# Keys straight into the split key stack, and the first two query stacks made on chip, in a one-core attention and feed-forward layer

## The chip, the cores and the metric

The kernel runs on one core of a Trainium2 chip. A core has a matrix engine (TensorE, PE in the profile; PEld is its weight load), a vector engine (VectorE, DVE), a scalar engine (ScalarE, ACT), a general engine (GpSimd, POOL) and a queue engine (SyncE, SP) that issues most DMA transfers. Matrix products are written to PSUM, eight banks of 128 partitions by 512 float32 values; everything else on chip lies in SBUF. The metric is the device time of one execution in microseconds (us); lower is better. Several runs of a kernel are told by their median.

## The reference

The input `x` is 4 sequences of 512 tokens with 1024 features. The layer is an attention block and a quantised linear layer, each behind a layer norm and with a residual sum:

```python
q = (ln(x) @ Wq).reshape(b, s, 32, 32)          # 32 heads of 32
k, v = split(ln(x) @ Wkv)                       # one key and one value head for all heads
scores = q @ k.T / sqrt(32) + slope[h] * (pos_k - pos_q)      # causal, -inf above
x = x + softmax(scores) @ v @ Wo
w = (six_bit_codes - zero_point) * scale        # 1024 x 1024
x = x + ln(x) @ w.T + bias
```

## The kernel before, in words

All products take float32 values split in a rounded part and a remainder ("hi" and "lo", type fp32r), so that a product of two values becomes two or three products on PE. ACT makes the rounded part by a copy, DVE the remainder by a subtraction; the helper `split` (L410 to L417) issues both.

A batch is one sequence. For each batch, `layernorm` normalises four token tiles, `chunk` transposes them into eight tiles `xc` of 128 features by 512 tokens and splits these. `keys_values` forms keys and values together: sixteen products into `pkv` (L616), whose partitions 0 to 63 hold the products with the rounded weights and 64 to 127 those with their remainders. It copies them to `y` (L623), transposes `y` back to tokens (L628), adds the two halves (L632, L636), makes three scaled columns of the key part (rounded, rounded, remainder; L643, L650), and transposes those once more (L660) into rows 0 to 95 of the key stack `kst` (L668). The values stay with tokens on partitions, as the right half of `kv`.

The 32 heads go in eight groups of four, one group a step, so 32 steps `i` over four batches. `queries` (L675) makes the 128 query rows of a group from 24 products into `pq` (L682) and splits them into `qh` and `ql`. It stores both to DRAM and loads them back (L420, helper `move`) as a stack `qs`: rows 0 to 31 rounded, 32 to 63 remainder, 64 to 95 rounded, the four heads side by side; rows 96 to 123 are prepared rows of the position bias, loaded from `qr_d`. One product of `qs` and `kst` then gives split scores with bias. `maxima` (L738, L751) forms scores with queries on partitions and takes row maxima on DVE with a custom instruction; sixteen a group. Its result is transposed (L767), split (L773, L778) and put into two more rows of `qs` by DMA. `attention` forms the scores again with keys on partitions (`st`, L819), takes exp on ACT (L829), zeroes the masked triangle on POOL (L838), multiplies with the values (`pav`, L848), sums the exponentials over key tiles on POOL (L860) and over keys on PE (`den`, L877). After all steps, `token_tile` does the output product (`po`, L1047), the second layer norm and the linear layer (`pf`, L1167) for sixteen tiles of 128 tokens.

PSUM's banks are shared out by name: two for `s`, two for `st`, one each for `av`, `den`, `q` and `misc`. `qs` has three buffers, the staging pool `stg` three.

The order of the work is not written out. Each operation is given with a due time (`at`), an estimated cost, and what it reads and writes; `Work.order` runs a list scheduler forward and backward several times over all engines, with a time per DMA and a penalty for shared ports, and the shortest order found is issued. `STEP` is 15.0 us per group in these due times, `T0` 16.0. A changed due time or dependence can therefore move any operation, far from the edit too. Every engine executes its own queue in order, and so does SP.

Of the kernel before, what the change touches and what calls it, by code (L numbers as in the profile page):

```python
# [32 lines left out]
F32 = mybir.dt.float32  # L33
# [5 lines left out]
ALU = mybir.AluOpType  # L39
# [302 lines left out]
def layer_kernel(  # L342
# [55 lines left out]
    def act(at, n, fn, out, ins, sbuf=False):  # L398
        work.op("ACT", at, n / 1.2 + (90.0 if sbuf else 70.0), fn, out, ins)
# [32 lines left out]

    ident = const([P, P], F32, "ident")
    make_identity(nc, ident())
    ident_r = const([P, P], F32R, "ident_r")
    nc.vector.tensor_copy(ident_r(), ident())
    neg_half = const([P, 1], F32, "neg_half")
    nc.gpsimd.memset(neg_half(), -0.5)

# [146 lines left out]
            [xt], [xt, nmr, rstd], sbuf=True,  # L586
        )

    FIRST = ("q", "misc", "s", "s", "st", "st", "av", "den")

    def chunk(at, b, c):

# [18 lines left out]
    def keys_values(at, b):  # L611
        pkv = new("ps_misc", "misc", [P, S], F32, f"pkv_{b}")
        for c in range(KC):
            def two(c=c):
                for s in range(2):
                    nc.tensor.matmul(  # L616
                        pkv(), wkv()[:, c, :], xc[b, c]()[:, s, :],
                        start=(c == 0 and s == 0), stop=(c == KC - 1 and s == 1),
                    )
            pe(at + 0.1 * c, [S, S], two, [pkv], [wkv, xc[b, c]])  # L620
        at += 1.0
        y = new("stg", "stg", [P, S], F32, f"y_{b}")
        act(at, S, lambda: nc.scalar.copy(y(), pkv()), [y], [pkv])  # L623
        tr = new("ps_misc", "misc", [P, NT, P], F32, f"trkv_{b}")
        for t in range(NT):
            pe(
                at + 0.1, [P + 95],
                lambda t=t: nc.tensor.transpose(tr()[:, t, :], y()[:, ts(t, P)], ident()),  # L628
                [(tr, t)], [y],
            )  # L630
        part = new("kv", "part", [P, NT, 2 * HD], F32, f"part_{b}")
        act(at + 0.2, 256, lambda: nc.scalar.copy(part(), tr()[:, :, 2 * HD :]), [part], [tr])  # L632
        t = kv[b] = new("kv", "kv", [P, NT, 2 * HD], F32, f"kv_{b}")
        dve(
            at + 0.3, 256,
            lambda: nc.vector.tensor_tensor(t(), tr()[:, :, 0 : 2 * HD], part(), ALU.add),  # L636
            [t], [tr, part],
        )
        tok = new("kv", "tok", [P, NT, 3 * HD], F32R, f"tok_{b}")
        for i in range(2):  # L640
            act(
                at + 0.4, P,
                lambda i=i: nc.scalar.activation(  # L643
                    tok()[:, :, ts(i, HD)], t()[:, :, 0:HD], AF.Copy, scale=SM_SCALE
                ),
                [(tok, i)], [t], sbuf=True,
            )
        dve(
            at + 0.5, P,
            lambda: nc.vector.scalar_tensor_tensor(  # L650
                tok()[:, :, ts(2, HD)], t()[:, :, 0:HD], SM_SCALE,
                tok()[:, :, 0:HD].bitcast(F32), ALU.mult, ALU.subtract,
            ),
            [(tok, 2)], [t, (tok, 0)], port=True,
        )
        trk = new("ps_misc", "misc", [P, S], F32R, f"trk_{b}")
        for j in range(NT):
            pe(
                at + 0.6, [P],
                lambda j=j: nc.tensor.transpose(  # L660
                    trk()[0 : 3 * HD, ts(j, P)], tok()[:, j, :], ident_r()
                ),
                [(trk, j)], [tok],
            )
        k = kst[b % 2]
        act(
            at + 0.7, S,
            lambda: nc.scalar.copy(k()[0 : 3 * HD, :], trk()[0 : 3 * HD, :].bitcast(F32)),  # L668
            [(k, "k")], [trk],
        )  # L670


    qs = {}

    def queries(at, i):  # L675
        b, g = divmod(i, NG)
        pq = new("ps_q", "q", [P, S], F32, f"pq_{i}")
        hi, lo = wq[g]
        for c in range(KC):
            def three(c=c):  # L680
                for n, (w, s) in enumerate(((hi, 0), (lo, 0), (hi, 1))):
                    nc.tensor.matmul(  # L682
                        pq(), w()[:, c, :], xc[b, c]()[:, s, :],
                        start=(c == 0 and n == 0), stop=(c == KC - 1 and n == 2),
                    )
            h = c // (KC // 2)
            pe(at + 1.3 * c, [S] * 3, three, [pq], [(hi, h), (lo, h), xc[b, c]], more=12.0)
        at += 10.4
        qh = new("q1", "qh", [P, S], F32R, f"qh_{i}")
        ql = new("q1", "ql", [P, S], F32R, f"ql_{i}")  # L690
        split(at, S, qh, ql, pq, qh, ql, pq)

        qs[i] = [(0, GH, new("qs", "qs", [P, GH, S], F32R, f"qs_{i}"))]
        for s, src in enumerate((qh, ql)):
            dma(
                at + 0.6 + 0.7 * s, 262e3,
                lambda s=s, src=src: move(q_d[i % 4, s], src()), [q_i[i % 4][s]], [src],
            )
# [27 lines left out]
    def maxima(at, i):  # L726
# [3 lines left out]
        for n, bank in enumerate(S_BANKS):  # L730
            ps = new("ps_s", "s", [P, S], F32, f"s_{i}_{n}")
            widths = [(t + 1) * P for t, _ in bank]
            places = [sum(widths[:m]) for m in range(len(bank))]

            def products(ps=ps, bank=bank, widths=widths, places=places):
                for (t, h), W, o in zip(bank, widths, places):
                    q, at = part(i, h)
                    nc.tensor.matmul(  # L738
                        ps()[:, o : o + W], q()[0:R_MAX, at, ts(t, P)], k()[0:R_MAX, :W],
                        start=True, stop=True,  # L740
                    )
            pe(
                at + 1.2 * n, widths, products, [ps],
                [(q, r) for q in {part(i, h)[0] for _, h in bank} for r in ROWS] + [k],
                more=5.0,
            )
            for (t, h), W, o in zip(bank, widths, places):
                junk = new("q1", "junk", [P, S], F32, f"junk_{i}_{t}_{h}")
                dve(
                    at + 1.2 * n + 0.3, W,  # L750
                    lambda ps=ps, junk=junk, t=t, h=h, W=W, o=o: nc.vector.tensor_tensor_reduce(  # L751
                        out=junk()[:, :W],
                        in0=ps()[:, o : o + W],
                        in1=mask()[:, S - W :],
                        scale=1.0,
                        scalar=-3e38,
                        op0=ALU.add,
                        op1=ALU.max,
                        accum_out=mx()[:, h * NT + t : h * NT + t + 1],
                    ),  # L760
                    [(mx, (t, h))], [ps], more=125.0,
                )
# [34 lines left out]
    def attention(at, i):  # L797
# [47 lines left out]
        def products(js):  # L845
            for j in js:
                for h in range(GH):
                    nc.tensor.matmul(  # L848
                        pav()[ts(h, HD), j * P :], kv[b]()[:, j, HD:], pr[j]()[:, h, :],
                        start=(j == 0), stop=(j == NT - 1), tile_position=(0, h * HD),  # L850
                    )
        for js, when in (((0, 1), 10.4), ((2, 3), 14.4)):
# [376 lines left out]
    for b in range(B):  # L1229
# [6 lines left out]
        for c in range(KC):  # L1236
            chunk(
                T - 4.0 + 0.5 * c if b == 0 else T - 0.9 * STEP + 1.3 * c - 2.6, b, c
            )
        keys_values(T + 6.0 if b == 0 else T - 1.0, b)  # L1240
        for g in range(NG):
            i = b * NG + g
            at = T0 + i * STEP
            queries(at, i)
            maxima(at + 17.0, i)
            attention(at + 34.0, i)
        invert(T + NG * STEP + 48.0, b)
    E = T0 + STEPS * STEP
    for c in range(KC):
        prep_wo(E - (NG - 1.2 - c) * STEP, c)  # L1250
    for kc in range(KC):
        load_codes(E - 2.0 + 0.5 * kc, kc)
    ffn_rows(E + 6.0, E + 46.0)
    for k in range(B * NT):
        token_tile(E + (-1.0, 11.0, 37.0)[min(k, 2)] + TILE * max(k - 2, 0), k, E + 25.0)

# [43 lines left out]
```

## Time and profile before

| | before |
|---|---|
| median of 3 runs | 827.22 us (826.88 to 828.23) |
| the profiled execution | 825.42 us |
| its span, first to last instruction | 823.5 us |
| PE busy | 795.9 us (97%) |
| DVE busy | 565.5 us (69%) |
| POOL busy | 514.1 us (62%) |
| ACT busy | 372.3 us (45%) |
| PE's share of the chain of waits | 89% |
| DMA queue of SP, share of 16 engines | 57.0% |

The profile is one execution recorded by the hardware. Busy times count instructions of an engine; matmuls are pipelined and their ends are modelled. In the slices the span is cut into 40 equal parts with a digit for the busy share in tenths. The view by stretches gives the same for chosen intervals. The timeline lists instructions by start; in square brackets stand the engine's idle time before an instruction and what ended it. The chain of waits goes back from the last instruction, at each step to what released it.

### The profile page before, as it was taken

What the parts mean: (1) busy time and instruction counts of PE and PEld (TensorE: products, weight loads), DVE (VectorE), ACT (ScalarE), POOL (GpSimd) and SP (SyncE); (2) the same over time, 40 slices, a digit from 0 to 9 for tenths busy, and PEclk for the clock granted to TensorE, in tenths of its full rate; (3) what the DMA queues carried; (4) which work ended last, traced back from release to release, by engine and by line L of the source; (5) the groups of instructions that cost most, each with busy time, mean ns of one, the idle gap of its engine ahead of it and who ended that gap; (6) DMA issues with size and microseconds to landing.
All of it is one profiled execution on the core that took longest, in us unless ns stands there. A gap on an engine that the chain in (4) does not pass through costs nothing.

```text
span 823.5 us, 13425 instructions
## 1 busy us (share of the span) xinstructions
PE 795.9 (97%) x4480; PEld 594.7 (72%) x4480; DVE 565.5 (69%) x1491; ACT 372.3 (45%) x659; POOL 514.1 (62%) x442
## 2 busy tenths in 40 slices
PE   5979999999999999999999999999999999999997
PEld 4756676777676767676775767667888888888885
DVE  7476777388786388777367675644998666666865
ACT  4336575464775445675556564330233323332320
POOL 4337977276787375877489896879465445554333
PEclk9989999999999999999999999999999999999999
DMA  7885853395553387543567966526875755665321
GB/s 223 245 252 154 232 164 91 111 266 188 155 145 100 106 262 211 148 120 111 174 174 194 235 189 208 170 58 171 214 178 158 173 131 129 152 151 137 97 52 51
DMA packets 131796, 133.39 MB, mean 162 GB/s; under 512 B 42964, under 2 KB 93140, under 8 KB 130704
## 3 DMA queue, kind: packets, MB, share of 16 engines
q1 hardware_dynamic: 130912, 129.01, 57.0%
q0 software_dynamic: 816, 3.53, 1.7%
q8 instruction: 35, 0.57, 0.3%
q14 instruction: 33, 0.27, 0.1%
HBM read 85.58 MB, written 39.85 MB: 152 GB/s over the span
## 4 chain that ended last, share of the span: by engine, by line
PE 89%; DVE 4%; DMA 2%; ACT 2%; issue 1%; POOL 1%; SPq 1%; DVEq 0%; ACTq 0%; POOLq 0%
PE po L1047 21%; PE pq L682 21%; PE pf L1167 13%; PE st L819 9%; PE s L738 9%; PE pav L848 8%; PE den L877 4%; PE pkv L616 2%; PE tr L598 2%; DVE junk L751 2%; ACT p L829 1%; POOL p L860 1%; DMA wo_st<-in_L_attn_Wo_dram 1%; DMA qs<-mt 1%; SPq L420 1%
## 5 line engine op out<-in xcount | busy, mean ns | idle before, releaser
L751 DVE CUSTOM_DVE_ANT_0 junk<-s,mask 128x384 f32<-128x384 f32 (+3 forms) x512 | 250.6, 490 | 119.6 <-PE s L738 88.8
L860 POOL TENSOR_TENSOR p<-p,p 128x1536 f32<-128x1536 f32 (+2 forms) x96 | 232.4, 2421 | 16.7 <-PE pav L848 15.0
L829 ACT ACTIVATE p<-st 128x512 f32<-128x512 f32 (+1 forms) x352 | 183.9, 559 | 115.8 <-PE st L819 110.7
L682 PE MATMUL pq<-xc,wqh 128*128 128x512 f32 x512 | 198.5, 405 | 2.3 <-DVE ql L415 1.4
L1047 PE MATMUL po<-woh,aT 128*128 128x512 f32 x512 | 164.8, 391 | 0.0
L838 POOL TENSOR_SCALAR_AFFINE_SELECT p<-p 128x512 f32<-128x512 f32 x128 | 82.2, 647 | 105.1 <-ACT p L829 104.3
L738 PE MATMUL s<-kst,qs 124*128 124x384 f32 (+3 forms) x512 | 127.5, 324 | 3.9 <-DVE mx L751 3.6
L819 PE MATMUL st<-qs,kst 126*128 126x512 f32 (+1 forms) x352 | 127.1, 399 | 3.9 <-ACT p L829 2.9
L1167 PE MATMUL pf<-wf,xT 128*128 128x512 f32 x512 | 121.1, 390 | 0.7 <-DVE xT L415 0.7
L738 PEld LDWEIGHTS s<-kst,qs 124*128 124x128 f32 x512 | 91.5, 189 | 34.2 <-DVE mx L751 8.9
L682 PEld LDWEIGHTS pq<-xc,wqh 128*128 128x128 f32 x512 | 97.7, 191 | 23.8 <-issue 2.7
L1047 PEld LDWEIGHTS po<-woh,aT 128*128 128x128 f32 x512 | 96.1, 188 | 21.7 <-DVE mx L751 0.8
L1167 PEld LDWEIGHTS pf<-wf,xT 128*128 128x128 f32 x512 | 95.8, 188 | 20.9 <-DVE xT L415 1.1
L682 PE MATMUL pq<-xc,wql 128*128 128x512 f32 x256 | 101.8, 398 | 0.1
L1047 PE MATMUL po<-wol,aT 128*128 128x512 f32 x256 | 99.7, 389 | 0.0
L819 PEld LDWEIGHTS st<-qs,kst 126*128 126x128 f32 x352 | 63.5, 190 | 25.7 <-ACT p L829 10.8
L848 PE MATMUL pav<-p,kv 128*32 128x512 f32 (+3 forms) x1024 | 79.9, 436 | 0.0
L848 PEld LDWEIGHTS pav<-p,kv 128*32 128x32 f32 x1024 | 29.6, 109 | 48.8 <-issue 37.6
L1187 POOL TENSOR_TENSOR x<-x,y 128x512 f32<-128x512 f32 x30 | 42.7, 1425 | 27.4 <-DVE y L1178 27.4
L1047 PEld LDWEIGHTS po<-wol,aT 128*128 128x128 f32 x256 | 48.1, 188 | 9.6
L538 POOL TENSOR_SCALAR rstd_f<-mv_f 128x1 f32<-128x1 f32 x16 | 3.9, 244 | 81.7 <-DVE mv_f L533 72.7
L682 PEld LDWEIGHTS pq<-xc,wql 128*128 128x128 f32 x256 | 49.2, 192 | 7.2 <-POOL wql L489 0.6
(92 smaller groups left out, 878.6 us busy)
## 6 DMA issues: line engine op xcount, KB each, us to landing
qs<-q_d SPq DMA_DIRECT2D x96, 256.0 KB
x<-_attn_hidden_states_dram SPq DMA_DIRECT2D x31, 512.0 KB
q_d<-qh SPq DMA_DIRECT2D x32, 256.0 KB
q_d<-ql SPq DMA_DIRECT2D x32, 256.0 KB
at_d<-a SPq DMA_DIRECT2D x32, 256.0 KB
raw<-at_d SPq DMA_DIRECT2D x16, 512.0 KB
raw<-rden_d SPq DMA_DIRECT2D x64, 128.0 KB
out_dram<-x SPq DMA_DIRECT2D x32, 256.0 KB
```

Of the source, the lines that this page charges most:

```text
L682: nc.tensor.matmul(pq(), w()[:, c, :], xc[b, c]()[:, s, :], start=(c == 0 and n == 0), stop=(c == KC - 1 and n == 2),)
L738: nc.tensor.matmul(ps()[:, o : o + W], q()[0:R_MAX, at, ts(t, P)], k()[0:R_MAX, :W], start=True, stop=True,)
L751: lambda ps=ps, junk=junk, t=t, h=h, W=W, o=o: nc.vector.tensor_tensor_reduce(out=junk()[:, :W], in0=ps()[:, o : o + W], in1=mask()[:, S - ...
L819: nc.tensor.matmul(ps()[:, place, :], k()[0:R_ALL, ts(j, P)], q()[0:R_ALL, mine, j * P :], start=True, stop=True,)
L829: lambda ps=ps, own=own, j=j: nc.scalar.activation(pr[j]()[:, own, :], ps(), AF.Exp),
L838: nc.gpsimd.affine_select(out=d, in_=d, pattern=[[0, GH], [1, P]], compare_op=ALU.is_ge, fill=0.0, base=0, channel_multiplier=-1,)
L848: nc.tensor.matmul(pav()[ts(h, HD), j * P :], kv[b]()[:, j, HD:], pr[j]()[:, h, :], start=(j == 0), stop=(j == NT - 1), tile_position=(0, ...
L860: nc.gpsimd.tensor_tensor(d, d, pr[j](), ALU.add)
L877: nc.tensor.matmul(d()[ts(h, HD), :], onesel()[:, g, :], pr[0]()[:, h, :], start=(g == 0), stop=(g == NG - 1), tile_position=(0, h * HD),)
L1047: nc.tensor.matmul(po(), aT[s][1]()[:, c, :], w()[:, ts(n, HALF)], start=(c == 0 and m == 0), stop=(c == KC - 1 and m == 2),)
L1167: nc.tensor.matmul(pf(), xT()[:, s, c, :], wf[c]()[:, ts(n, HALF)], start=(c == 0 and s == 0), stop=(c == KC - 1 and s == 1),)
L1187: (nc.vector if last else nc.gpsimd).tensor_tensor(d, d, y(), ALU.add)
```

## The change

Keys: the two halves of `pkv` are added at once (ACT copies the lower half's partner to partitions 0 to 63, DVE adds), with features still on partitions. From that sum ACT writes the two scaled rounded row blocks of `kst` and DVE the remainder block. The transposes now serve the values alone and are due four microseconds later; the second set of transposes and the fp32r identity are gone. Keys of the first batch are due ahead of its first queries (`T - 1.0` in place of `T + 6.0`).

Queries: for steps 0 and 1 (`DIRECT = 2`) `pq` lies in the banks `av` and `den`, and a new function `stack_here` fills `qs` from it: per head two ACT copies of 32 rows by 512 and one DVE subtraction. The two stores and three loads of those steps go away; the bias rows are loaded earlier. Their scores wait by head rather than for the whole stack, and `maxima` and `attention` of these steps get earlier due times. The banks in which the first batch's `chunk` transposes are reordered to fit. The row loads of the linear layer get earlier due times.

```diff
-    ident_r = const([P, P], F32R, "ident_r")
-    nc.vector.tensor_copy(ident_r(), ident())
...
-    FIRST = ("q", "misc", "s", "s", "st", "st", "av", "den")
+    FIRST = ("av", "misc", "s", "s", "st", "st", "q", "den")
...
-        act(at, S, lambda: nc.scalar.copy(y(), pkv()), [y], [pkv])
...
+        act(at, S, lambda: nc.scalar.copy(y()[0 : 2 * HD], pkv()[2 * HD :]), [y], [pkv])
+        dve(
+            at + 0.1, S,
+            lambda: nc.vector.tensor_tensor(
+                y()[0 : 2 * HD], pkv()[0 : 2 * HD], y()[0 : 2 * HD], ALU.add
+            ),
+            [y], [y, pkv],
+        )
+        k = kst[b % 2]
+        for i in range(2):
+            act(
+                at + 0.2 + 0.2 * i, S,
+                lambda i=i: nc.scalar.activation(
+                    k()[ts(i, HD), :], y()[0:HD], AF.Copy, scale=SM_SCALE
+                ),
+                [(k, i)], [y], sbuf=True,
+            )
+        dve(
+            at + 0.3, S,
+            lambda: nc.vector.scalar_tensor_tensor(
+                k()[ts(2, HD), :], y()[0:HD], SM_SCALE, k()[0:HD, :].bitcast(F32),
+                ALU.mult, ALU.subtract,
+            ),
+            [(k, 2)], [y, (k, 0)], port=True,
+        )
+        tr = new("ps_misc", "misc", [P, NT, 2 * HD], F32, f"trkv_{b}")
         for t in range(NT):
             pe(
-                at + 0.1, [P + 95],
-                lambda t=t: nc.tensor.transpose(tr()[:, t, :], y()[:, ts(t, P)], ident()),
+                at + 4.0, [P + 60],
+                lambda t=t: nc.tensor.transpose(
+                    tr()[:, t, :], y()[0 : 2 * HD, ts(t, P)], ident()[0 : 2 * HD, 0 : 2 * HD]
+                ),
                 [(tr, t)], [y],
             )
...
+        v = kv[b] = new("kv", "kv", [P, NT, HD], F32, f"kv_{b}")
+        act(at + 4.5, P, lambda: nc.scalar.copy(v(), tr()[:, :, HD:]), [v], [tr])
...
+    DIRECT = 2
+
+    def stack_here(at, i, pq):
+        g = i % NG
+        q = new("qs", "qs", [P, GH, S], F32R, f"qs_{i}")
+        qs[i] = [(0, GH, q)]
+        dma(
+            at - 8.0, 229e3, lambda: move(q()[R_BIAS:R_MAX, :, :], qr_d[g]), [(q, "b")], [qr_i[g]]
+        )
+        for h in range(GH):
+            src = ts(h, HD)
             act(
+                at + h, S, lambda h=h, src=src: nc.scalar.copy(q()[0:HD, h, :], pq()[src, :]),
+                [(q, (0, h))], [pq],
+            )
+            dve(
+                at + 0.6 + h, S,
+                lambda h=h, src=src: nc.vector.tensor_tensor(
+                    q()[ts(1, HD), h, :], pq()[src, :], q()[0:HD, h, :].bitcast(F32), ALU.subtract
                 ),
+                [(q, (1, h))], [pq, (q, (0, h))],
+            )
+            act(
+                at + 0.5 + h, S,
+                lambda h=h, src=src: nc.scalar.copy(q()[ts(2, HD), h, :], pq()[src, :]),
+                [(q, (2, h))], [pq],
+            )
 
     def queries(at, i):
         b, g = divmod(i, NG)
-        pq = new("ps_q", "q", [P, S], F32, f"pq_{i}")
+        p = ("av", "den")[i] if i < 2 else "q"
+        pq = new("ps_" + p, p, [P, S], F32, f"pq_{i}")
...
+        if i < DIRECT:
+            stack_here(at, i, pq)
+            return
...
-        keys_values(T + 6.0 if b == 0 else T - 1.0, b)
+        keys_values(T - 1.0, b)
...
-            maxima(at + 17.0, i)
-            attention(at + 34.0, i)
+            first = i < DIRECT
+            maxima(at + (8.0 if first else 17.0), i)
+            attention(at + (22.0 if first else 34.0), i)
...
-    ffn_rows(E + 6.0, E + 46.0)
+    ffn_rows(E + 0.0, E + 34.0)
```

More of the change, by code (lines that the diff above doesn't have):

```diff
@@ L622, in keys_values @@
         y = new("stg", "stg", [P, S], F32, f"y_{b}")
-        act(at, S, lambda: nc.scalar.copy(y(), pkv()), [y], [pkv])
-        tr = new("ps_misc", "misc", [P, NT, P], F32, f"trkv_{b}")
+        act(at, S, lambda: nc.scalar.copy(y()[0 : 2 * HD], pkv()[2 * HD :]), [y], [pkv])
[7 more added lines that the diff above has]
+        k = kst[b % 2]
@@ L625, in keys_values @@
+        tr = new("ps_misc", "misc", [P, NT, 2 * HD], F32, f"trkv_{b}")
         for t in range(NT):
             pe(
-                at + 0.1, [P + 95],
-                lambda t=t: nc.tensor.transpose(tr()[:, t, :], y()[:, ts(t, P)], ident()),
+                at + 4.0, [P + 60],
+                lambda t=t: nc.tensor.transpose(
+                    tr()[:, t, :], y()[0 : 2 * HD, ts(t, P)], ident()[0 : 2 * HD, 0 : 2 * HD]
+                ),
                 [(tr, t)], [y],
             )
-        part = new("kv", "part", [P, NT, 2 * HD], F32, f"part_{b}")
@@ L632, in keys_values @@
[L632 to L637, printed above, removed]
-        )
-        tok = new("kv", "tok", [P, NT, 3 * HD], F32R, f"tok_{b}")
-        for i in range(2):
-            act(
-                at + 0.4, P,
-                lambda i=i: nc.scalar.activation(
-                    tok()[:, :, ts(i, HD)], t()[:, :, 0:HD], AF.Copy, scale=SM_SCALE
+        v = kv[b] = new("kv", "kv", [P, NT, HD], F32, f"kv_{b}")
@@ new lines, in keys_values @@
+        act(at + 4.5, P, lambda: nc.scalar.copy(v(), tr()[:, :, HD:]), [v], [tr])
+    qs = {}
+    DIRECT = 2
[5 more added lines that the diff above has]
+            at - 8.0, 229e3, lambda: move(q()[R_BIAS:R_MAX, :, :], qr_d[g]), [(q, "b")], [qr_i[g]]
+        )
+        for h in range(GH):
+            src = ts(h, HD)
+            act(
+                at + h, S, lambda h=h, src=src: nc.scalar.copy(q()[0:HD, h, :], pq()[src, :]),
[5 more added lines that the diff above has]
+                    q()[ts(1, HD), h, :], pq()[src, :], q()[0:HD, h, :].bitcast(F32), ALU.subtract
@@ L645, in keys_values @@
                 ),
-                [(tok, i)], [t], sbuf=True,
+                [(q, (1, h))], [pq, (q, (0, h))],
             )
[L648 to L663, printed above, removed]
-            )
[L665 to L673, printed above, removed]
+            act(
+                at + 0.5 + h, S,
+                lambda h=h, src=src: nc.scalar.copy(q()[ts(2, HD), h, :], pq()[src, :]),
+                [(q, (2, h))], [pq],
+            )
@@ L743, in maxima @@
                 at + 1.2 * n, widths, products, [ps],
-                [(q, r) for q in {part(i, h)[0] for _, h in bank} for r in ROWS] + [k],
+                [
+                    (part(i, h)[0], (r, h) if i < DIRECT and r != "b" else r)
+                    for _, h in bank for r in ROWS
+                ] + [k],
                 more=5.0,
@@ L848, in products @@
                     nc.tensor.matmul(
-                        pav()[ts(h, HD), j * P :], kv[b]()[:, j, HD:], pr[j]()[:, h, :],
+                        pav()[ts(h, HD), j * P :], kv[b]()[:, j, :], pr[j]()[:, h, :],
                         start=(j == 0), stop=(j == NT - 1), tile_position=(0, h * HD),
```

## The prediction

> **What bounds the kernel now.** The first view is the head of the page: busy shares, then the slices.
>
> ```profile
> PE 795.9 (97%) x4480; PEld 594.7 (72%) x4480; DVE 565.5 (69%) x1491; ACT 372.3 (45%) x659; POOL 514.1 (62%) x442
> PE   5979999999999999999999999999999999999997
> PEclk9989999999999999999999999999999999999999
> ```
>
> TensorE (PE) is busy 97% of the span and the chain of waits gives it 89%, so time can only come from PE work that goes away, from PE idling, or from its clock. The slices put all but a little of the last two into the first three. The view by stretches, cut at the events of the head, sizes them (columns: stretch, its length, PE, PEld, DVE, ACT and POOL busy, granted PE clock, DMA share, GB/s).
>
> ```profile
> 0.00:8.04 8.04, 0.00 (x0) 0.00 (x1) 3.97 (x9) 0.70 (x1) 3.22 (x20) 1.00 0.75 260
> 8.04:16.06 8.02, 6.91 (x32) 6.28 (x33) 6.77 (x14) 4.85 (x8) 4.58 (x9) 1.00 0.86 224
> 16.06:30.00 13.94, 13.94 (x66) 11.54 (x67) 8.84 (x13) 7.73 (x16) 4.45 (x4) 1.00 0.60 162
> 30.00:41.65 11.65, 9.86 (x44) 7.32 (x43) 6.14 (x22) 3.96 (x7) 4.32 (x4) 1.00 1.04 313
> 41.65:60.70 19.05, 13.60 (x48) 9.79 (x49) 14.43 (x51) 7.17 (x11) 7.41 (x13) 0.88 0.90 251
> 60.70:75.00 14.30, 14.30 (x83) 10.30 (x82) 7.86 (x29) 9.67 (x18) 8.29 (x8) 0.92 0.51 117
> ...
> 44.20:45.90 1.70, 0.33 (x2) 0.18 (x2) 1.67 (x6) 0.26 (x1) 0.00 (x0) 0.98 1.04 289
> 45.90:47.60 1.70, 1.70 (x4) 1.41 (x5) 1.70 (x5) 0.00 (x0) 0.24 (x2) 0.50 1.09 298
> 47.60:49.30 1.70, 1.70 (x5) 1.34 (x4) 1.56 (x5) 0.86 (x2) 0.98 (x3) 0.51 1.10 372
> 49.30:51.00 1.70, 1.70 (x9) 1.39 (x8) 0.00 (x0) 0.91 (x1) 1.61 (x4) 1.00 0.97 342
> ```
>
> Before 16.06 PE waits for the input and the layer norm, which the change leaves alone. From 16.06 to 60.70 PE idles 1.79 + 5.45 = 7.24 us; from 60.70 to 75 not at all, and from 75 to 545 only 5.2 us in 470. The clock falls to half for 3.4 us twice (from 45.9, and likewise from 59.5), which costs 1.7 each, 3.4 us. So 7.24 + 3.4 = 10.64 us stand in the head.
>
> Why PE idles there is in the timeline (start, length, engine, line, tile).
>
> ```profile
> 21.83 0.59 ACT L412 CAST qh<-pq 128x512 fp32r<-128x512 f32 x1 [1.58 <-PE pq L682]
> 26.63 0.99 SPq L420 DMA_DIRECT2D qs<-q_d  x2
> 29.58 0.58 ACT L668 CAST kst<-trk 96x512 fp32r<-96x512 f32 x1 [0.94 <-PE trk L660]
> 34.62 0.63 PE L738 MATMUL s<-kst,qs 124*128 124x512 f32 x2
> 35.06 0.69 DVE L751 CUSTOM_DVE_ANT_0 junk<-s,mask 128x512 f32<-128x512 f32 x1 [1.98 <-PE s L738]
> 45.23 0.27 PE L767 MATMUL trm<-ident,mx 128*16 128x128 f32 x1 [1.68 <-DVE mx L751]
> 57.93 0.68 PE L819 MATMUL st<-qs,kst 126*128 126x512 f32 x2
> ```
>
> The first queries are done at 21.8, the keys at 30.2, yet the first scores start at 34.62: the query halves travel to DRAM and back (issues at 22.45 to 28.84). Then VectorE (DVE) takes the maxima of a group in 9.3 us (35.06 to 45.00, 0.69 of other work taken off), during which PE has little else. The second groups of exp products (st) can start only at 57.93. This is the filling of a pipeline that PE bounds once it is full.
>
> **Part by part.**
>
> *Keys.* PE loses the four trk transposes of each batch. The chain gives them 0.24 us, times 4 batches 0.96. The four trkv transposes, 0.44 in the chain, shrink to a 64-row input and 64 columns: between no saving and the 0.24 of trk; I take 0.1 a batch, 0.4. Together 1.36 us of PE work, nearly all in the part where PE is never idle. ACT: y 0.59 stays; part 0.37, two tok 0.30 and kst 0.58 (1.55) become two stack copies of 512 columns (0.59 each) and the value copy (at most 0.37): 1.55 again. DVE: kv 0.43 and tok 0.29 become two 512-column steps of 0.69: +0.66 a batch, hidden by PE in batches 1 to 3 (DVE 69% busy). If that cover were gone it would be 2.6. The identity's second copy (0.56 on DVE at 1.40) lies in a wait for the input: nothing.
>
> *Order of the start.* The x splits end on DVE at 20.2. Keys' sums, two products (0.46) per chunk, then end at about 20.7; DVE's 0.60 a chunk is slower than PE's 0.46, so PE loses between 0 (the first queries fill in) and 1.0; I take 0.5. Then 0.59 + 0.69 + 0.59 + 0.69 and hand-offs: keys stand at 23.4, or at 26.8 if the weight unpacking that DVE runs at 20.11 to 23.58 stays ahead of them. Sums and first queries are 3.63 + 5.73 of PE work from 16.06: 25.4 to 25.9. Either date of the keys is covered by that.
>
> *Query stacks.* No row has a 32x512 copy. The nearest are 16x128 (0.25 us) and 96x512 (0.58); the 128x512 one is 0.59. Length, not partitions, moves these, so 0.59 is taken; the ends are 0.25 and 0.62. A group goes from one ACT copy and one DVE subtraction to eight (4.7 us) and four (2.8 us). Added in two groups: ACT 14 x 0.59 = 8.2, DVE 6 x 0.69 = 4.1 us. ACT is busy 3.96 of 11.65 us at 30 to 41.65, so it hides 8.2 over 25 to 40; queued behind are weight casts (L487), whose products start later. Each head needs only its own rows, so the first scores wait for two ACT copies and one subtraction beside the second: 25.9 + 1.4 = 27.3, bounds 26.7 and 28.5, against 34.62. Ten transfers of 256 KB (2.6 MB, 8 us at the 313 GB/s seen here) leave a stretch with a DMA share of 1.04. The bias-row loads stay, moved up; the second waits on SP for a row block that GpSimd issues at 23.23 and that lands 4.8 later (median). Weight loads queue behind it, needed at about 33: nothing, or up to 3 us if they come that late.
>
> The Trainium skill, PSUM — Partial Sum Buffer, section "PSUM bank collisions raise a hardware error", says two engines must not read one bank and quadrant together. The second ACT copy and the subtraction of a head do just that. No row of this kernel does it; if they were kept apart, the first group would be late by up to 2.8 us (estimate, four subtractions of 0.69), and 7.8 below would be about 5.
>
> *DVE after that.* From 27.3 to the end of the second group's maxima: 2 x 9.3, seven stack subtractions 4.8, two query splits 1.4, small maxima 0.5, statistics of batch 1 6.1 (now at 41.5 to 49.2): 31.4, ending at 58.7, or 52.6 if the statistics wait; before 61.99. PE's supply in those 31.4 us: the rest of the second queries 4.1, three more groups of queries 16.5, two groups of scores 4.8, exp products 2.4, value products 2.4, sums 1.0: 31.2. Supply and DVE's pace just balance, so I leave 2.0 us of idling and one half-clock stretch.
>
> The clock row needs a word. The Trainium skill, TensorE: Matmul & The Clock Gate, section "Why this matters for your kernels", has the clock fall after PE-idle gaps of over some 3 us. Here no gap after 16.06 exceeds 1.68 us, and it fell twice, after 3.4 us with PE busy 0.83 (42.5 to 45.9) and about 2.0 (56.1 to 59.5). By the page the 3.4 us would not be there to win, and the gain would be 6.1; the rows decide.
>
> *The rest.* Later batches keep their order but for the keys; value transposes come 4 us later, with nobody waiting until the value products some 14 us on. The longer life of y holds one staging buffer. Row loads for the feed-forward part come 6 and 12 us sooner in plan; waits on them are 1.2 and 0.7 us off PE. Nothing each; a reshuffled order can move the 5.2 us of later idling by some 1.5 either way.
>
> **Sum.** Of 10.64 us, 0.5 + 2.0 + 1.7 = 4.2 stay: 6.4 gained, plus 1.36: 7.8. The profiled execution took 825.42 (span 823.5), so 817.6; the median of the runs is 1.80 above it: 827.22 - 7.8 = 819.4.
>
> **Rivals.** A: DVE bounds the whole filling. Batch 1's statistics and 4.1 us of subtractions sit ahead of the second maxima, PE idles 5.0 us and both half-clock stretches remain: 8.4 stays, 2.2 + 1.36 = 3.6 gained, 823.6. For it: DVE is busy 14.43 of 19.05 from 41.65. Against: it does 6.14 of 11.65 before, and the statistics are not needed for 60 us.
>
> B, slower: PE waits on DVE in crumbs all along the filling, and the clock gate punishes it. With 8.0 us idle and four half-clock stretches of 1.7, 14.8 is lost in place of 10.64; less 1.36 the time rises 2.8 to 830.0. It decides once idling and clock after 16.06 pass 12.0. For it: two stretches follow a half-idle PE already. Against: that needs more idling than now, from an earlier start.
>
> C, no change: the lead is given back later, to 827. Against: PE idles 1% from 75 to 545, so there is no slack to swallow it.
>
> **Numbers.** Forecast 0.66, A 0.17, B 0.12, C 0.05. A measurement of this kernel tells about 0.2%, 1.65 us, from no change. A ends faster but for 0.02, the forecast always: faster 0.81, same 0.07, slower 0.12. Full recovery, 10.64 + 1.36 = 12.0, gives 815.2, the lower end with a little for order: 815.0. The upper end takes in A and late starts: 826.5.
>
> **What would show it.** Right: first scores at about 27, first exp products before 50, one or no half-clock stretch, PE idle after 16.06 near 2.5 us, no trk rows, 32x512 copies of 0.59. Wrong: scores at 27 but maxima still ending near 62 (A), three or more rows at clock 0.5 (B), new PE idling after 75 (C).

## The result, and the profile after

The change made the kernel slower: a median of 832.82 us (832.05 to 833.5, 4 runs) against 827.05 us for the kernel before in the same session, a ratio of 1.0072 with a 95% interval of 1.005 to 1.0093. The profiled execution took 832.68 us with a span of 830.8 us, 7.3 us more than the span of before.

The head of the page, with busy shares and slices, answers to the first view of the prediction.

```profile
PE 802.8 (97%) x4464; PEld 593.2 (71%) x4464; DVE 588.5 (71%) x1496; ACT 377.3 (45%) x669; POOL 524.9 (63%) x442
PE   5988999999999999999999999999999999999997
PEclk9989899999999999999999999999999999999999
```

PE executes 16 instructions fewer and is busy 6.9 us longer. A second slice of low clock has come, the fifth (83 to 104 us), where the kernel before had none. DVE is busy 23 us longer. The view by stretches tells more; the first four lines have the cuts of the prediction.

```profile
16.06:30.00 13.94, 13.23 (x59) 10.10 (x58) 9.16 (x15) 8.55 (x16) 4.59 (x4) 1.00 0.45 118
30.00:41.65 11.65, 11.28 (x52) 8.41 (x50) 9.47 (x35) 6.99 (x13) 3.00 (x3) 1.00 0.37 89
41.65:60.70 19.05, 15.74 (x70) 11.19 (x69) 12.86 (x43) 10.71 (x21) 5.47 (x7) 0.82 0.55 159
60.70:75.00 14.30, 13.65 (x98) 8.63 (x99) 12.46 (x28) 8.54 (x15) 13.29 (x10) 1.00 0.91 248
75.00:100.00 25.00, 22.14 (x90) 13.43 (x88) 16.18 (x57) 15.24 (x25) 19.13 (x26) 0.86 0.79 216
...
465.00:480.00 15.00, 12.96 (x77) 7.76 (x76) 10.24 (x23) 7.31 (x14) 12.10 (x8) 0.89 0.58 167
```

The same view of the kernel before, for the two later stretches:

```profile
75.00:100.00 25.00, 24.50 (x154) 16.70 (x153) 18.88 (x66) 14.15 (x29) 23.32 (x20) 1.00 0.91 261
465.00:480.00 15.00, 15.00 (x93) 11.06 (x92) 9.97 (x37) 10.56 (x23) 13.81 (x10) 1.00 0.75 211
```

Length less PE's busy time is PE's idle time; the clock column shows the half-clock stretches, which begin at 44.4 (6.8 us long), 81.9, 92.1 and 474.4 (3.4 us each). Half of their length is lost.

| us lost to idling + clock | 16 to 75 | 75 to 165 | 165 to 405 | 405 to 560 | after 560 |
|---|---|---|---|---|---|
| before | 7.2 + 3.4 | 0.9 + 0 | 2.8 + 0 | 1.6 + 0 | 0.7 + 0 |
| after | 5.0 + 3.4 | 3.4 + 3.4 | 1.4 + 0 | 3.9 + 1.7 | 0.5 + 0 |

The head gained 2.2 us; 75 to 165 lost 5.9 and 405 to 560 lost 4.0. The timeline shows what became of the first scores (chosen rows: start, length, engine, line, tile; the idle time before in brackets).

```profile
22.96 0.68 DVE L641 SCALAR_TENSOR_TENSOR kst<-y,kst 32x512 fp32r<-32x512 f32 x1 [0.36 <-ACT kst L634]
24.99 1.16 ACT L673 CAST qs<-pq 32x512 fp32r<-32x512 f32 x2 [0.65 <-PE pq L697]
27.51 0.68 DVE L678 TENSOR_TENSOR qs<-pq,qs 32x512 fp32r<-32x512 f32 x1 [0.64 <-ACT qs L685]
27.53 0.50 PE L756 MATMUL s<-kst,qs 124*128 124x512 f32 x1
28.23 0.58 ACT L673 CAST qs<-pq 32x512 fp32r<-32x512 f32 x1 [0.75 <-DVE qs L678]
40.94 1.17 ACT L673 CAST qs<-pq 32x512 fp32r<-32x512 f32 x2
42.15 0.68 DVE L678 TENSOR_TENSOR qs<-pq,qs 32x512 fp32r<-32x512 f32 x1 [0.89 <-ACT qs L673]
42.89 0.50 PE L756 MATMUL s<-kst,qs 124*128 124x512 f32 x1 [1.20 <-DVE qs L678]
44.66 1.41 DVE L678 TENSOR_TENSOR qs<-pq,qs 32x512 fp32r<-32x512 f32 x2
45.50 1.49 PE L756 MATMUL s<-kst,qs 124*128 124x512 f32 x2 [2.11 <-DVE qs L678]
50.54 0.74 PE L840 MATMUL st<-qs,kst 126*128 126x512 f32 x1
```

Scores start at 27.53 in place of 34.62 and exp products at 50.54 in place of 57.93. But ACT's copies and DVE's subtractions of one PSUM tile go in turns: ACT waits 0.75 behind a subtraction at 28.23, and the subtraction at 42.15 waits 0.89 behind two copies. PE then waits 3.3 us for the subtractions of the second stack, and the clock halves at 44.4. Further on, again in chosen rows:

```profile
60.30 3.60 POOL L881 TENSOR_TENSOR p<-p,p 128x1536 f32<-128x1536 f32 x1
60.48 3.69 DVE L940 TENSOR_SCALAR v<-qw 128x256 int32<-128x256 int32 x1
78.50 0.49 PE L756 MATMUL s<-kst,qs 124*128 124x512 f32 x1 [0.33 <-DVE mx L772]
467.38 3.49 POOL L881 TENSOR_TENSOR p<-p,p 128x1536 f32<-128x1536 f32 x1
467.67 4.28 DVE L415 TENSOR_TENSOR aT<-raw,aT 128x1024 fp32r<-128x1024 f32 x1 [0.74 <-ACT aT L412]
472.61 0.50 PE L756 MATMUL s<-kst,qs 124*128 124x512 f32 x1 [2.03 <-DVE mx L772]
```

Twice a DVE instruction that reads SBUF started just behind a POOL sum and lasted until that had ended: 3.69 us in place of 0.40 (the like unpacking at 60.23) and 4.28 in place of 1.22 (below). After the second PE waits 2.03 us for the maxima queued behind it.

### The profile page after: what moved, and what is told of

Same layout as the page of the kernel before. It is cut to its first block, busy times and chain, and to the rows that moved or that the text cites. A ratio compares the mean times of both kernels' runs of the same rounds, so it can differ in the third digit from the quotient of the medians.

```text
span 830.8 us, 13410 instructions
## 1 busy us (share of the span) xinstructions
PE 802.8 (97%) x4464; PEld 593.2 (71%) x4464; DVE 588.5 (71%) x1496; ACT 377.3 (45%) x669; POOL 524.9 (63%) x442
## 4 chain that ended last, share of the span: by engine, by line
PE 78%; DVE 7%; DMA 6%; POOL 3%; ACT 2%; issue 2%; SPq 1%; DVEq 0%; POOLq 0%; ACTq 0%
PE pq L697 18%; PE po L1068 17%; PE pf L1188 12%; PE st L840 9%; PE s L756 8%; PE pav L869 6%; PE den L898 3%; DVE junk L772 2%; DMA raw<-rden_d 2%; PE pkv L614 2%; PE tr L596 2%; DMA qs<-q_d 1%; DMA qs<-mt 1%; DMA q_d<-ql 1%; POOL raw L1045 1%
## 5 line engine op out<-in xcount | busy, mean ns | idle before, releaser
L697 PE MATMUL pq<-xc,wqh 128*128 128x512 f32 x512 | 201.9, 407 | 0.8 <-DVE xc L415 0.6
L756 PE MATMUL s<-kst,qs 124*128 124x384 f32 (+3 forms) x512 | 129.8, 329 | 8.9 <-DVE mx L772 4.0
L1208 POOL TENSOR_TENSOR x<-x,y 128x512 f32<-128x512 f32 x30 | 52.1, 1738 | 38.4 <-DVE y L1199 38.3
L1119 ACT COPY halves<-x 128x1024 uint16<-128x1024 uint16 x24 | 23.9, 1044 | 64.9 <-DVE x L1089 64.9
```

What stands on the lines that cost most here:

```text
L697: nc.tensor.matmul(pq(), w()[:, c, :], xc[b, c]()[:, s, :], start=(c == 0 and n == 0), stop=(c == KC - 1 and n == 2),)
L756: nc.tensor.matmul(ps()[:, o : o + W], q()[0:R_MAX, at, ts(t, P)], k()[0:R_MAX, :W], start=True, stop=True,)
L1208: (nc.vector if last else nc.gpsimd).tensor_tensor(d, d, y(), ALU.add)
```

## The experiments

The theories named in the expectations: **D**, the new stacks overfill DVE, and its other work is pushed into 60 to 95 us. **R**, later **O**: the planner deals every engine a new order for any edit, and that alone is worth several us. **T**: the turns on the PSUM bank. **P**: the port that DVE and POOL share. Ratios are to the kernel before in the same session, where its median was 826.05 (e1 to e4), 827.67 (e5 to e8), 827.14 (e9 to e12), 827.52 (e13 to e16) and 826.48 (e17, e18).

### Parts of the change: e1, e2, e3

e1 keeps the key path and sends all query stacks by DRAM again, with the old bank order and row dates:

```diff
-    DIRECT = 2
+    DIRECT = 0
...
-    ffn_rows(E + 0.0, E + 34.0)
+    ffn_rows(E + 6.0, E + 46.0)
```

> The kernel before with the new key path and the earlier key date alone; query stacks, their dates and the row loads as before. Theory D (the two direct query stacks fill VectorE's queue, so its other work is pushed into 60 to 95 us and costs the time): no loss here, 825 to 828, since 0.9 us of trk transposes go and no stack subtractions come. Theory R (the order is reshuffled as a whole, and where GpSimd's port-holding operations meet VectorE's is chance): 822 to 833, PE idling and half-clock stretches at other places than in either kernel.

831.74 us, 1.0076 (1.0056 to 1.0095). e2 keeps the two stacks and gives the keys their old path, transposes and dates, and the row loads their old dates (the old key code is left out here):

```diff
...
-        keys_values(T - 1.0, b)
+        keys_values(T + 6.0 if b == 0 else T - 1.0, b)
...
-    ffn_rows(E + 0.0, E + 34.0)
+    ffn_rows(E + 6.0, E + 46.0)
```

> The kernel before with the two direct query stacks and their dates alone; keys by two sets of transposes and due at their old time, row loads as before. Theory D: most of the loss is here, 831 to 835, with VectorE over 85% busy somewhere between 60 and 95 us and PE idle there. Theory R: 822 to 833, with no fixed place of the loss.

837.06, 1.0133 (1.0113 to 1.0152). e3 is the change with the old row dates alone:

```diff
-    ffn_rows(E + 0.0, E + 34.0)
+    ffn_rows(E + 6.0, E + 46.0)
```

> The changed kernel with the old due times of the row loads of the linear layer. These belong to the end of attention, so the first 400 us should not care. Theory D: 830 to 834, with the same loss at 60 to 95 us. Theory R: even this edit moves the order from the start on, so that stalls in the first 120 us change by over 2 us.

836.34, 1.0137 (1.0119 to 1.0155). Every part alone is slower than before, e3 by more than the whole. e1 has no stack on chip, and D gave it 825 to 828; it lost as much as the whole, which D does not explain. e3 has the order of the changed kernel on PE up to 413 us, and there it is 3.0 us ahead, with 3.4 us less lost to the clock; in other order at the end of the attention it lost all of that and more. Such parts can't be added up, so what follows keeps orders fixed.

### Turns and order, first try: e4 to e8

e4 makes the second copy of a head from the first one in SBUF, so that ACT reads the bank once a head:

```diff
-                lambda h=h, src=src: nc.scalar.copy(q()[ts(2, HD), h, :], pq()[src, :]),
-                [(q, (2, h))], [pq],
+                lambda h=h: nc.scalar.copy(q()[ts(2, HD), h, :], q()[0:HD, h, :].bitcast(F32)),
+                [(q, (2, h))], [(q, (0, h))], sbuf=True,
```

> The changed kernel, but the second rounded copy of each head is taken from the first one in SBUF and not from the PSUM tile, so that ScalarE and VectorE need not take turns on one PSUM tile. In the changed kernel a stack takes 24.99 to 32.64, 7.6 us, with 0.75 of ScalarE idling at each turn. Expected of a stack here: about 5 us if the turns were the cost, 7 or more if not. Time: theory D gives 829 to 832 (2 us less waiting in the head); theory R anything from 823 to 835.

825.05, 0.9994 (0.9975 to 1.0014): some 6.5 us recovered, but the planner had dealt a new order too. The first stack took 6.2 us (25.15 to 31.38), where 7.6 stood in the change and 5 were expected without turns. e5 and e6 (e6 with e4's copies) hold the planned dates of the kernel before, with new operations at the dates of those that they replace:

```diff
-    def order(self, rounds=4, passes=6):
+    KEPT = (...)   # the dates of before's plan
+    def order(self):
+        ...        # one forward pass on these dates
```

> The changed kernel with one difference: the list scheduler makes a single forward pass, in which every operation that the kernel before has too gets the priority and the buffer order of the plan of the kernel before, and the 44 new operations those of the ones they replace (keys' sums ahead of the first queries). From about 300 us on the order is then nearly that of before. Theory R (the loss is a worse order far from the edit, above all at the end of attention): the late idling goes and the time falls to 822 to 826. Theory D (VectorE's work in the head): PE idling and half-clock stretches at 60 to 95 us stay, 830 to 833.

844.75, 1.0203 (1.0176 to 1.023), the slowest of all and outside the ranges of both theories. The timeline of e5 shows where part of that goes (its lines are numbered otherwise; L1480 is the subtraction L415):

```profile
555.46 2.54 POOL L2273 TENSOR_TENSOR x<-x,y 128x512 f32<-128x512 f32 x2
557.96 2.38 POOL L1946 TENSOR_TENSOR p<-p,p 128x1024 f32<-128x1024 f32 x1
560.31 2.47 POOL L2231 TENSOR_TENSOR x<-x,rows 128x512 f32<-128x512 f32 x2
...
555.88 9.21 DVE L1480 TENSOR_TENSOR aT<-raw,aT 128x1024 fp32r<-128x1024 f32 x1
565.14 1.22 PE L2133 MATMUL po<-woh,aT 128*128 128x512 f32 x2 [4.93 <-DVE aT L1480]
```

A subtraction of 1.2 us lasted 9.21 while POOL ran one sum after another, and PE waited 4.93. Dates that were good for one set of operations were not good for another here.

> As the order-kept kernel, and the second rounded copy of each head taken from the first in SBUF, so that a stack no longer takes turns on PSUM. If the turns cost 2 to 3 us in the head: 2 to 3 us less than the order-kept kernel, 819 to 824. If PE had other work under them: the same time within 1.5.

831.2, 1.0058 (1.0036 to 1.0081), far below e5 but above the 819 to 824 expected, with a wait of 5.8 us at 582 of PE's `pf` on DVE's `xT`. e7 gives the kernel *before* only the row dates of the change, which adds no work:

```diff
-    ffn_rows(E + 6.0, E + 46.0)
+    ffn_rows(E + 0.0, E + 34.0)
```

> The kernel before with the new due times of the row loads and nothing else: no work is added or removed. Theory R: the order of the end of attention is moved, and the time by 2 to 8 us either way, with no difference in the first 300 us. Theory D: within 1.5 us of before.

830.6, 1.0042 (1.0024 to 1.006): a neutral edit costs 3.5 us. e8 tests D: the statistics of batch 1 read 64 columns in place of 512, with every engine's order that of the changed kernel:

```diff
-                lambda i=i: nc.vector.bn_stats(st()[:, i, :], xt()[:, ts(i, HALF)]),
+                lambda i=i: nc.vector.bn_stats(
+                    st()[:, i, :], xt()[:, i * HALF : i * HALF + (64 if name[:2] == "a1" else HALF)]
+                ),
```

> The changed kernel in exactly its order, but the layer norm statistics of the second batch read 64 columns of each half instead of 512 (about 0.5 us less on VectorE for each of eight, 4 us, at 65 to 88 us in the changed kernel). Theory D: PE's idling at 75 to 95 us (2.5 us) and the two half-clock stretches there (3.4 us) shrink, and 3 to 5 us go. Theory R: under 1.5 us go.

833.11, 1.0072 (1.0049 to 1.0095), as the change. PE waits at 77 to 81 as before, so the length of the statistics is not what holds PE there. D falls for the statistics.

### The same orders, written out: e9 to e12

Here `order` returns a fixed list, so each pair differs in one thing alone:

```diff
+    ORDER = (...)
     def order(self):
+        return [self.ops[n] for n in self.ORDER]
```

> Every engine's instructions stand in exactly the order of the changed kernel (the list of operations is written out in place of the planner); the one edit is that the second ScalarE copy of a head in the two new query stacks reads the first copy in SBUF, not the PSUM sums, so ScalarE no longer takes turns with VectorE's subtraction on the bank. Theory T, the turns cost the time: PE's waits at 42.9 to 45.5 us (3.3 us, all on that subtraction) go to about 1, and with them part of the half-clock stretch of 6.8 us at 44.4: 832.8 falls by 2.5 to 5, to 828 to 830. Theory O, the copy version won 7 us because the planner gave it another order all along: here the order is the changed kernel's, so 831 to 833 stays, with the waits at 77 to 81 us and at 472 us as they were.

> The converse: the order of the version with copies from SBUF (825.05 us) written out for all engines, but the second copies read PSUM again, as in the change. Theory T: the turns come back, PE waits on the subtractions of the second stack grow by 2 to 3 us at 40 to 46 us: 827.5 to 830. Theory O: the order decides, 825 to 826.5. The two kernels with copies from PSUM then differ by order alone (against 832.8), and so do the two with copies from SBUF.

| ratio to before | second copy from PSUM | from SBUF |
|---|---|---|
| order of the change | 1.0072 (1.005 to 1.0093) | e9: 1.0052 (1.0033 to 1.0071) |
| order of e4 | e12: 1.0028 (1.0 to 1.0056) | e4: 0.9994 (0.9975 to 1.0014) |

Across, the turns: 0.0020 and 0.0034, or 1.7 and 2.8 us; the intervals of each pair overlap, the sign is the same. Down, the order: 0.0044 and 0.0058, or 3.6 and 4.8 us; the intervals of the second pair lie apart. So O is shown, and it weighs more. T is likely, but these times alone do not show it: e9 won less than the 2.5 us expected, and PE's waits on the subtractions fell from 3.3 only to 2.7 us, not to 1. In e12 the same waits rose from e4's 1.8 to 3.6. e10 exchanges two neighbouring POOL instructions of the changed kernel at 467 us:

```diff
 # POOL's order
-p<-p,p (sum)    wol<-wo_st,woh
+wol<-wo_st,woh  p<-p,p (sum)
```

> The changed kernel with its order written out, and one pair of GpSimd instructions exchanged near 467 us: the sum of products (3.49 us) that started 0.3 us ahead of VectorE's subtraction aT now stands behind the 1.2 us weight subtraction that followed it. Nothing else moves on any engine. Theory P, the shared port costs the time there: VectorE's subtraction falls from 4.28 to 1.2 to 2.5 us, PE's wait of 2.03 us at 472.6 goes, and the half-clock stretch behind it (1.7 us) with it: 829 to 831. Against it: if PE's wait there has another cause or the time is lost again behind it, 832 to 833.

830.51, 1.0027 (1.0013 to 1.0041), 3.7 us less than the change. In its timeline:

```profile
472.15 1.22 DVE L415 TENSOR_TENSOR aT<-raw,aT 128x1024 fp32r<-128x1024 f32 x1 [0.74 <-ACT aT L412]
472.72 1.81 POOL L487 TENSOR_TENSOR wol<-wo_st,woh 128x512 fp32r<-128x512 f32 x1 [0.83 <-ACT woh L485]
474.50 5.99 POOL L881 TENSOR_TENSOR p<-p,p 128x1536 f32<-128x1536 f32 x2
```

The subtraction takes 1.22 us, and PE has no wait on the maxima behind it. PE's instructions have one order in both kernels, so the two profiles can be set side by side: e10's, the slowest of its executions (834.92), stands 4.5 us behind the change's at 459 us and 0.4 behind at 479. P holds there: one exchange is worth more than half of the whole loss. e11 has e9's copies, this exchange and one near 60 us (a DMA issue ahead of the sum at 60.30):

> The order of the changed kernel, with the second copies from SBUF, the exchange near 467 us, and one more exchange on GpSimd near 60 us: a DMA issue goes ahead of the sum of products (3.60 us) that held VectorE's unpacking for 3.69 us. If turns and port each cost what theories T and P say, the gains add: 2.5 to 5 and 2 to 3.7, so 824 to 828, about the time before the change. The exchange near 60 frees VectorE for 3.3 us; if the waits at 77 to 81 us (1.9 us) come from VectorE being late, they go too; a run with shorter statistics did not move them, so I expect them to stay. Theory O: 829 to 833.

829.95, 1.003 (1.0016 to 1.0043). The exchange at 467 is worth less here than in e10 (0.0022 against e9, intervals overlapping). The one at 60 did not free the unpacking: its record now starts at 59.79, 0.36 us ahead of the sum's, and still lasts 4.11 us. PE waits 1.3 us on maxima behind it, up to 100 us, as before. So what the 3.69 us at 60.48 cost stays open.

### Design or deal: e13, e15, e16

e13 and e16 give e4 and the kernel before the same neutral dates:

```diff
-    ffn_rows(E + 0.0, E + 34.0)
+    ffn_rows(E + 3.0, E + 40.0)
```

> The version with copies from SBUF (825.05 us), with one edit that has nothing to do with the change: the planner is told to load the feed-forward rows 3 and 6 us later (E + 3, E + 40), and so deals out another order from somewhere in the first 100 us on. Theory O (which order the planner deals is worth several us, whatever the edit): 828 to 832. If the version is better by design and its order is not special: within 1.7 us of 825.

> The kernel before with the same neutral edit (E + 3, E + 40 in place of E + 6, E + 46): a second deal of its planner. Theory O: slower than before by 2 to 5 us, 829 to 832, as with the first such edit (830.6). Against it: within 1.7 us of 827.

e13 took 837.82, 1.013 (1.0114 to 1.0145), more than O expected; at 75 to 110 PE waits 2.3 us on `wql` and 1.7 on `wqh`, weight halves that were dealt late. e16 took 828.5, 1.0022 (1.0002 to 1.0043), less than its expectation. e15 makes only the first stack on chip:

```diff
-    DIRECT = 2
+    DIRECT = 1
```

> The version with copies from SBUF, but only the first group's stack is made by ScalarE and VectorE; the second goes by DRAM as before the change (7 ScalarE copies and 3 subtractions fewer at 37 to 46 us). If the second stack's work on VectorE is what holds PE at 41 to 46 us, the idling at 16 to 75 falls below the 4.3 us of that version, to about 3, unless the DRAM way delays the second scores beyond 41. The planner deals a new order, so the total has the spread of theory O: 823 to 831; read the head from its own stretch.

833.07, 1.0069 (1.0054 to 1.0085). Its total is spoilt at 560 to 600 us, where one wait on DVE takes 4.2. At 16 to 75 PE idles 4.5 us, not the 3 expected; but from 75 to 100 it does not idle at all, and at 100 and 165 e15 is the furthest ahead, as the next table shows. The table is an estimate from one profile of each kernel: each PE instruction is credited with the mean start-to-start time of its kind over the profiles, and the entry is how far a kernel is ahead of the one before at that time, in us of PE work. With medians in place of means the entries at 75 move by some 3 us, so small differences should not be read.

| lead at | 45 | 75 | 100 | 165 | 460 | 540 | 600 |
|---|---|---|---|---|---|---|---|
| after | 0.5 | 2.2 | -4.9 | -4.2 | -1.3 | -4.7 | -8.5 |
| e3, old row dates | 0.5 | 3.5 | -3.0 | -1.1 | 0.0 | -1.7 | -11.0 |
| e4, copies from SBUF | 1.0 | 2.5 | -3.0 | -2.8 | 1.9 | 0.3 | -1.0 |
| e13, e4 with neutral dates | 0.9 | 2.0 | -6.2 | -6.1 | -4.1 | -5.2 | -13.4 |
| e15, one stack | 0.2 | 1.4 | 2.8 | 3.8 | 1.3 | -0.8 | -9.9 |
| e7, before, neutral dates | 0.0 | 3.3 | 0.3 | -0.7 | 1.6 | -1.7 | -4.6 |
| e16, before, neutral dates | 0.1 | 3.7 | 1.7 | 2.3 | 4.5 | 1.9 | -3.8 |
| e18, moved by hand | 2.1 | 4.0 | -1.8 | -1.2 | 3.5 | 1.0 | 0.7 |

Two things can be read off. First, all four deals of the whole change lose 5.5 to 8.2 us between 75 and 100, the kernel before in other deals 2.0 and 3.0, and the version with one stack nothing; e2, with both stacks but late keys, fell from 1.5 to 0.1. Counted as idling and clock, these four lose 4.3 to 9.1 us there, e1 0.9, e2 1.2, e15 nothing. So in the planner's deals the loss goes with early keys and a second stack on chip together, and the head's lead is gone by 100 us. It is not bound to them: e5 has both, under kept dates, and loses 1.0 us there to idling and clock, against 6.3 in the change. An order by hand for e15 was not tried. Second, between 460 and 600 the deals differ by far more than the change brings, on both sides. e7 and e16 show, too, that some 3.5 of the 10.64 us which I saw lost in the head come back to the kernel before by 75 us with another deal alone.

### Mended by hand: e14, e17, e18

e14 takes e4's order and moves operations in the list: four first copies of the second stack in a row, two maxima ahead of its subtractions, the split of the third queries 6 us earlier, two chunks of the fourth queries between the scores, one ACT cast behind the exponentials at 87, and the exchange at 467. e17 leaves that exchange out. e18 is e17 with the last chunk of the third queries ahead of the second stack's first score, and a third chunk of the fourth queries between the scores.

```diff
 # ACT, second stack: copies (row block, head); qh_2 of the third queries
-(0,0) (0,1) (2,0) (2,1) (0,2) (0,3) (2,2) (2,3) qh_2
+(0,0) (0,1) (0,2) (0,3) (2,0) (2,1) qh_2 (2,2) (2,3)
 # DVE: maxima, subtractions of the stack, ql_2 of the third queries
-max sub0 max max sub1 max sub2 max sub3 max ... ql_2
+max max max sub0 sub1 max ql_2 sub2 max sub3 max ...
 # PE: scores of the second stack, chunks of the fourth queries
-s1 s2 s3
+s1 pq_3[0] s2 pq_3[1] s3
 # e18 besides
-s0 pq_2[7] ... s4 s5
+pq_2[7] s0 ... s4 pq_3[2] s5
```

> The order of the version with copies from SBUF, written out, and a few operations moved by hand. At 37 to 48 us: ScalarE makes the four first copies of the second stack in a row; VectorE's split of the third queries, which holds their PSUM bank to 48.7, comes 6 us earlier; two chunks of the fourth queries (0.70 us each) fill PE's waits between the scores. At 87: ScalarE's cast of unpacked codes (1.05 us) goes behind the exponentials. At 467: the exchange on GpSimd. Theory T/D (what is left of the loss in the head is the turn of VectorE and ScalarE at the stacks, with PE out of other work): PE's 4.3 us idle at 16 to 75 falls to 2 to 3, 1 us is won at 87, and part of the 6.8 us half-clock stretch: 821 to 823.5, faster than the kernel before. If PE only runs out of filling work later instead: 824 to 826.

> The hand-moved version of e14 without its exchange on GpSimd near 467 us; the moves in the head and at 87 stay. In e14 that exchange cost time: against the planner's order of e4 the stretch between the 27th and the 29th maxima transpose grew from 33.5 to 35.2 us, with ScalarE's exponentials waiting for GpSimd's late sum. If so, 1.5 to 2 us are won: 821 to 822.5. If the exchange was neutral, 823 to 824.

> e17 with two further moves in PE's order: the last chunk of the third queries goes ahead of the second stack's first score (which waits 0.67 us there), so that their split starts 0.9 us earlier, and a third chunk of the fourth queries goes between the scores at 46 us (0.70 us into waits of 1.5). If PE lacks work there, 0.5 to 1.5 us below e17; if the chunk is only missed later, at 50 to 56 us, the same as e17 within 1 us.

e14 took 823.72, 0.9951 (0.9932 to 0.997); e17 825.13, 0.9998 (0.9977 to 1.0018); e18 822.26, 0.9953 (0.9936 to 0.997). e14 and e18 beat the kernel before by 0.5%. That kernel had no such moves made by hand, so the change can be made to pay, but what it is worth between two orders of equal care is not shown. The clock row of e18's slices:

```profile
PEclk9999999999999999999999999999999999999999
```

PE's waits of e18 from 16 to 75 us (total, times, longest):

```profile
PE pq L697 <- DVE ql L415: 0.8, 1, 0.8
PE s L756 <- DVE mx L772: 0.6, 2, 0.4
PE s L756 <- ACT qs L685: 0.6, 1, 0.6
...
PE s L756 <- DVE qs L678: 0.2, 1, 0.2
```

The wait on the subtractions, 3.3 us in the change and 1.8 in e4, has gone to 0.2, and no half-clock stretch is left before 88 us. PE idles 3.2 us at 16 to 75 in place of 4.3 in e4, so PE did lack work there, in part. e17 missed its expectation: its profiled execution has the shortest span of all (820.7, clock 0.999), yet its ratio is 0.0047 over e14's, with granted clocks from 0.991 to 0.999 in its runs. Why that order meets the half clock more often I can't say, and what the exchange at 467 is worth in this order stays open.

## Why the prediction was wrong, by its own steps

It forecast 7.8 us gained; the profiled spans show 7.3 lost (the medians 5.8), 15.1 apart. Three terms failed: the turns on the PSUM bank, taken at no cost; the balance in the head, which was to leave 4.2; and the 1.5 for a reshuffled order.

**Right.** Keys stood at 23.64 (23.4), first scores at 27.53 (27.3), 32x512 copies took 0.57 to 0.58 us (0.59), the second group's maxima were done by 57.5, when their transpose ran (58.7). Exp products began at 50.54, half a us later than the "before 50" of the forecast.

**Keys, the trkv term.** The 0.4 us never came: sixteen transposes of 64x64 took 1.6 us from start to start, the 128x128 ones 1.4. The sixteen of `trk` had taken 1.1. So 1.0 in all in place of 1.36.

**Query stacks, the turns.** The step that took no cost for two engines on one bank failed. ACT's eight copies of the first stack took 6.9 us (24.99 to 31.92) in place of 4.7, and those of the second, with the subtractions, 8.2 (37.86 to 46.07). The Trainium skill, PSUM — Partial Sum Buffer, section "PSUM bank collisions raise a hardware error", spoke against the change here, and my estimate beside it, 2.8 us, has the size of what the runs show for both stacks (1.7 and 2.8, each pair with overlapping intervals). That is luck in part: I made it for the first group, whose scores were not late, and PE's waits fell on the second stack. That page lets engines read different 32-partition quadrants of a bank together; here the copy of the third head at 28.23 waited on the subtraction of the second (27.51), so on another quadrant: the turns went by the whole bank. The trace shows a wait on a semaphore, which is how this program keeps the engines apart; what would happen without it no run here shows.

**The term "4.2 to stay".** In the head 5.0 us of idling and 3.4 of clock stayed, 8.4, where supply and DVE's pace were to balance at 2.0 and 1.7. That 8.4 is rival A's figure is luck in part. A's cause holds in part: DVE's queue is what PE waits for, but at the second stack's subtractions, and not for the statistics, which the planner had put at 65 us and later (e8).

**C, the lead given back.** I gave it 0.05, since PE idled 1% from 75 to 545 and had no slack. That argument failed: a PE that comes early meets the same row of scores, each 0.85 us behind the maxima, with no other product in its queue, and it begins to idle. From 75 to 165 such waits (1.8 us on the maxima), some others and two half-clock stretches took 6.8 us where before lost 0.9. That the order dealt leaves PE there without other products is argued from e5, which lost 1.0 us from 75 to 100; no run changed that row alone.

**"A reshuffled order can move the later idling by some 1.5 either way."** This was the worst term. Four deals of the whole change, e4's copies included, lie from 0.9994 to 1.0137, three deals of the kernel before from 1.0 to 1.0042. I knew that a due time moves any operation and still sized this by the idling left in one order. From 405 to 560 the change lost 4.0 us more than before, and e10 took back as much between 459 and 479 with one exchange.

**B, slower,** came nearest: crumbs of waiting, four half-clock stretches, 830.0 forecast. But its nearness is luck in part: the filling, where B put all 14.8 us of loss, lost 8.4, with one stretch of 6.8 us, and the other three stretches came behind it.

The 15.1 us: 4.2 in the head, 5.9 from 75 to 165, 4.0 from 405 to 560, 0.4 of work not saved, less 2.3 won elsewhere (1.4 from 165 to 405, 0.2 after 560, 0.7 at both ends), and 2.9 that I can't split, where PE counts as busy but follows other engines, as with the last exponentials at 545 to 548.

## What to carry to other kernels

Where a planner decides the order, an edit is one draw from its orders: apply one or two neutral edits to both kernels, or write the order out, before a difference of 1% is put down to a change. Time won while a pipeline fills is kept only if the queue of the bounding engine holds other work at every later wait; look for the first row of products that goes at another engine's pace. And when a new step reads one PSUM bank from two engines, cost it as if they took turns.

## What the runs showed of the hardware

A DVE instruction waiting for POOL is not always let in when POOL's current instruction ends: in e5 it waited through six in a row, 9.21 us for 1.2. The Trainium skill, SBUF — State Buffer, section "SBUF: two separate sides", says that who starts first holds the shared pair for its whole instruction; the 3.69 and 4.28 us rows agree, but by that rule alone I would expect the 9.21 to end some 2 us on, after the instruction that POOL had begun. Nor does e11 fit it, where the record of the unpacking starts ahead of the sum's and yet lasts 4.11 us, unless a record's start is not where an instruction takes the port.

The clock halved with no long gap ahead of it. PE was busy 1.19, 2.17, 2.52 and 1.78 us of the 3.4 us before the four stretches of the changed kernel, and its longest wait near them was 2.11 us. The prediction weighed the Trainium skill, TensorE: Matmul & The Clock Gate, section "Why this matters for your kernels", which warns of PE-idle gaps over some 3 us; the rows speak against that limit here as they did before. No threshold follows from them either: in e18 PE was busy 2.45 of the 3.4 us up to 44.4 and no stretch followed, while 2.90 of the 3.4 us up to 88.0 were followed by one.

Small pieces cost what large ones do: a 32x512 copy took 0.58 us against 0.57 to 0.59 for 128x512, and four 64x64 transposes 0.39 us against 0.36 for four of 128x128 in the same place. Between the middle ones the step did fall, from 0.11 to 0.06 us, but the step to the next product rose from 0.03 to 0.15.
